# A causal-attention kernel on one core: the 512-column score product of heads 0 and 1 cut into 128 and 384 columns in all visits with a diagonal pair and one long product

## The chip, the cores and the metric

The kernel runs on one core of one Trainium2 chip. The metric is the device time of one execution in microseconds (us): the median of several runs. A core has these engines: TensorE for matrix products (PE, with its weight loads PEld), VectorE (DVE), ScalarE (ACT), GpSimd (POOL), and SyncE (SP), which issues transfers.

## The reference

The input x has 32 batches of 256 channels with 32 x 32 = 1024 tokens, in float32. Each batch is normalized over groups of 8 channels, projected to q, k and v of 8 heads with 32 channels each, and attended causally with the diagonal masked too; the result is added to x.

```python
q = einsum('oc,bcs->bos', q_w, xn) + q_b        # xn: x normalized by groups of 8 channels
k, v = split(einsum('oc,bcs->bos', kv_w, xn) + kv_b)
scores = einsum('bhqd,bhkd->bhqk', q, k) / sqrt(32)
attn = softmax(where(mask == 0, -10000, scores)) # mask: key strictly before query
out = x + einsum('bhqk,bhkd->bhqd', where(mask == 0, 0, attn), v)
```

## The kernel before

**Batches, groups, visits.** The 8 heads are two groups of four; a group's four heads lie in the four 32-row strips of a 128-row tile of q and of k. The 1024 tokens are 8 blocks of 128. For one batch and one group the causal half of the score matrix is cut into 6 visits (the table `VISITS`); a batch so has 12 visits, numbered v = 0 to 11, with the group g and the place i in the table as quotient and rest of v by 6. All 32 batches give 384 visits. A visit makes two sorts of score products, for keys on the rows of PSUM and queries on the columns:

- *long* ones, up to 512 columns, that need no mask. Visits 1 to 4 have one long product of 512 columns; visits 0 and 5 have two, of 384 and 128 columns.
- *short* ones. In visits 0, 1, 3 and 4 (the table `PAIRS`) this is a pair of diagonal blocks, in two phases: one of 128 columns and one of 64. In visits 2 and 5 it is one product of 256 columns.

**One row of products.** A product of one head has 32 rows of the array for its 32 channels. Each is made in two halves of 64 keys, which go to PSUM partitions 0 to 63 and 64 to 127. A row of the order of instructions, with "x4" at its end, is the product of two heads in both halves. Heads 0 and 1 are one pair and heads 2 and 3 the other: the two pairs lie in different strips of the array. As a product is in float32, the trace has two loads and two matmuls for it, which are called its two passes below; four records of the PE for each product.

**The order of a visit** is written by hand in `scores`, since all engines run under a manual schedule. With one long product and a pair of blocks it is: the short products of heads 2 and 3, the long one of heads 0 and 1, the long one of heads 2 and 3, a wait of PE for the semaphore `bank_free` (the short products of heads 2 and 3 have ended, whose PSUM banks the next write), and the short products of heads 0 and 1. Two lists set the first part:

- `begin` holds the calls that make the long products of heads 0 and 1. Where the visit is in the table `SPLIT` and the batch isn't the last, it holds two calls of `part_of`, for columns 0 to 127 and 128 to 511 of the one long product. `SPLIT` is compared with v, so it names visits 3 and 4 of group 0 alone.
- where `begin` has more than one call, its first is made between the two phases of the short products of heads 2 and 3, and these two phases come in reverse: 64 columns, the first call, 128 columns.

Behind the scores, PE makes a projection of this or the next batch (`project_qk` with tile `pp`, `project_v` with tile `ppv`) and then the products with v of the visit before (`values`, tile `acc`). ScalarE takes the exponential of the three pairs of PSUM banks (`sT`) into `e` and `eh`, GpSimd masks the diagonal blocks, VectorE adds up the exponentials by key. PSUM holds the score tiles three deep, two banks each, so each visit writes the banks that the visit before it wrote.

## Time and profile before

| | us |
|---|---|
| median of 3 runs (lowest, highest) | 1791.58 (1791.32, 1792.56) |
| span of the profiled execution, first to last instruction | 1791.2 |
| TensorE busy | 1782.1 (99%) |
| VectorE busy | 1669.4 (93%) |
| ScalarE busy | 1441.4 (80%) |
| GpSimd busy | 897.9 (50%) |

The page gives the span of the profiled execution and no separate time of its own; the span is 0.4 us less than the median of the runs. The granted clock of TensorE is 0.999 of the full one over the span. A line such as "912.56 1.46 PE L329 MATMUL sT<-q,k 32*64 32x64 f32 x56" of the timeline says: from 912.56 us on and for 1.46 us, 56 matmuls of line 329 one behind another, which write the tile sT from q and k, the first of them with 32 rows by 64 columns of weights and 64 streamed columns. Ends of matmuls are modelled, so the end of a row overlaps the next one; the starts don't. The time from the start of one sT row to the start of the row behind it is called the length of a section of scores here.

### The profile page before, as it was taken

To read this page: it belongs to the slowest core of one execution; us is meant where nothing else is said; L and a number is where in the kernel's file an instruction comes from. 1 tells how busy PE (TensorE), PEld (TensorE's weight loads), DVE (VectorE), ACT (ScalarE), POOL (GpSimd) and SP (SyncE) were. 2 spreads that over 40 slices of the span, in tenths; PEclk is the share of its full clock that TensorE was granted. 3 is DMA by queue.
4 is the path that set the end of the run, shared out by engine and by line. 5 is a ranking of instruction groups with operands and counts; after the bars stand their busy time and mean duration, and the time that the engine had idled before them with its cause. 6 is when DMAs were issued, how large, how long until landed. Compare 5 with 4: busy or idle time off the path is not lost.

```text
span 1791.2 us, 81784 instructions
## 1 busy us (share of the span) xinstructions
PE 1782.1 (99%) x37036; PEld 936.1 (52%) x37036; DVE 1669.4 (93%) x1796; ACT 1441.4 (80%) x1928; POOL 897.9 (50%) x935
## 2 busy tenths in 40 slices
PE   9999999999999999999999999999999999999998
PEld 5555555555555555555555555555555555555554
DVE  4689999999999999999999999999999999999998
ACT  6888878888778788788887888877888878888785
POOL 2355554554555555545555555454455554554542
PEclk9999999999999999999999999999999999999999
DMA  2567766767677676676776676767766766777663
GB/s 72 105 117 142 137 133 135 148 138 147 128 142 138 137 141 138 132 144 142 142 138 134 137 142 138 150 129 140 139 145 131 141 136 135 149 138 141 133 109 98
DMA packets 92771, 240.21 MB, mean 134 GB/s; under 512 B 26272, under 2 KB 27792, under 8 KB 76544
## 3 DMA queue, kind: packets, MB, share of 16 engines
q0 software_dynamic: 17360, 100.58, 40.1%
q1 hardware_dynamic: 74912, 134.28, 25.9%
q8 instruction: 290, 4.75, 1.1%
q14 instruction: 65, 0.53, 0.1%
q10 hardware_dynamic: 144, 0.07, 0.0%
HBM read 69.90 MB, written 34.95 MB: 59 GB/s over the span
## 4 chain that ended last, share of the span: by engine, by line
PE 99%; DVE 0%; ACT 0%; issue 0%; POOL 0%; POOLq 0%
PE sT L329 31%; PE acc L451 28%; PE pp L173 27%; PE ppv L173 13%; PE pd L503 1%; PE busy L159 0%; PE wt L152 0%; ACT e L426 0%; DVE rb_last L576 0%; DVE rb_last L563 0%; DVE turned L560 0%; DVE acc L573 0%; DVE inv_last L562 0%; POOL ident masks.py:199 0%; PE pv L173 0%
## 5 line engine op out<-in xcount | busy, mean ns | idle before, releaser
L426 ACT ACTIVATE e<-sT 128x1024 f32<-128x1024 f32 x768 | 744.3, 1022 | 301.5 <-PE sT L329 298.8
L366 POOL TENSOR_SCALAR_AFFINE_SELECT diagonal<-eh 128x512 f32<-128x512 f32 x512 | 563.3, 1122 | 625.4 <-ACT eh L422 624.7
L469 DVE TENSOR_TENSOR e<-e,e 128x1024 f32<-128x1024 f32 x314 | 578.0, 1841 | 23.0 <-ACT v L293 3.5
L329 PE MATMUL sT<-q,k 32*64 32x64 f32 (+1 forms) x18928 | 577.9, 367 | 0.1
L329 PEld LDWEIGHTS sT<-q,k 32*64 32x64 f32 x18928 | 397.0, 131 | 203.8 <-PE sT L329 67.4
L173 PE MATMUL pp<-xn,wT 128*32 128x512 f32 x4096 | 492.3, 598 | 0.0
L451 PE MATMUL acc<-e,v 128*32 128x512 f32 (+3 forms) x4608 | 401.0, 450 | 0.0
L422 ACT ACTIVATE eh<-sT 128x768 f32<-128x768 f32 (+1 forms) x384 | 341.6, 890 | 0.0
L451 PEld LDWEIGHTS acc<-e,v 128*32 128x32 f32 x4608 | 149.2, 110 | 261.5 <-issue 239.0
L173 PE MATMUL ppv<-wT,xn 128*32 128x256 f32 x4096 | 247.5, 382 | 0.0
L469 DVE TENSOR_TENSOR diagonal<-diagonal,e 128x1536 f32<-128x1536 f32 x126 | 194.5, 1544 | 16.1 <-PE acc L451 6.5
L173 PEld LDWEIGHTS pp<-xn,wT 128*32 128x32 f32 x4096 | 107.0, 109 | 195.8 <-issue 163.7
L469 DVE TENSOR_TENSOR e<-e,eh 128x1024 f32<-128x1024 f32 x126 | 177.6, 1410 | 6.5
L451 PEld LDWEIGHTS acc<-diagonal,v 128*32 128x32 f32 x4096 | 120.9, 110 | 88.1 <-issue 68.2
L173 PEld LDWEIGHTS ppv<-wT,xn 128*32 128x32 f32 x4096 | 120.2, 109 | 80.0 <-issue 7.0
L469 DVE TENSOR_TENSOR e<-e,diagonal 128x2048 f32<-128x2048 f32 x63 | 144.0, 2285 | 18.9 <-POOL diagonal L366 18.7
L451 PE MATMUL acc<-diagonal,v 128*32 128x128 f32 x4096 | 158.9, 273 | 0.0
L205 POOL DMA_INDIRECT eight<-each,group_of x31 | 42.9, 1383 | 193.4 <-DMA each<-st 193.4
L262 ACT ACTIVATE xn<-x,shift,rstd 128x256 f32<-128x256 f32 x248 | 137.2, 614 | 0.8 <-POOL shift L247 0.8
L576 DVE SCALAR_TENSOR_TENSOR rb<-num,v_bias_col,x 128x256 f32<-128x256 f32 x248 | 121.5, 530 | 4.4
L482 POOL DMA_DIRECT2D e<-e x124 | 103.6, 835 | 42.6 <-issue 42.6
L482 POOL DMA_DIRECT2D diagonal<-diagonal x124 | 105.1, 847 | 0.7
(87 smaller groups left out, 1092.2 us busy)
## 6 DMA issues: line engine op xcount, KB each, us to landing
x<-in_x_dram SPq DMA_DIRECT2D x124, 256.0 KB, 3.8
diagonal<-diagonal POOLq DMA_DIRECT2D x62, 512.0 KB, 6.1
e<-e POOLq DMA_DIRECT2D x62, 512.0 KB, 5.7
rb<-inverses SPq DMA_DIRECT2D x124, 256.0 KB, 4.0
out_dram<-rb SPq DMA_DIRECT2D x124, 256.0 KB, 4.2
diagonal<-diagonal POOLq DMA_DIRECT2D x62, 256.0 KB, 4.6
folded<-diagonal SPq DMA_DIRECT2D x62, 256.0 KB, 5.1
e<-e POOLq DMA_DIRECT2D x62, 256.0 KB, 4.6
```

What stands on the lines that cost most here:

```text
L173: nc.tensor.matmul(out[part], lhsT=lhsT[:, part], rhs=rhs, start=start, stop=stop, skip_group_check=True)
L205: nc.gpsimd.indirect_dma_start(eight, None, live["each", b].rearrange("(m c) s -> m (c s)", c=CPG), bass.IndirectOffsetOnAxis(ap=group_of[ ...
L262: nc.scalar.activation(to, of, AF.Identity, bias=live["shift", b][:, g : g + 1], scale=rstd)
L329: return nc.tensor.matmul(bank[c : c + KEYS, cols], lhsT=live["k", b, g][rows, kb * P + c : kb * P + c + KEYS], rhs=live["q", b, g][rows, ...
L366: nc.gpsimd.affine_select(out=square[:, :, place + s * P : place + (s + 1) * P], in_=raw[:, :, (1 - s) * KEYS : (3 - s) * KEYS], pattern=[ ...
L422: exp = nc.scalar.activation(eh.rearrange("p (n bank) q -> p bank n q", n=2)[:, :, :, :narrow], short[:, :, :, :narrow], AF.Exp)
L426: nc.scalar.activation(e[:, 2 * a : 2 * a + 2, :wide], pairs[a][:, :, :wide], AF.Exp)
L451: nc.tensor.matmul(acc[HD * j : HD * (j + 1), of], lhsT=live["v", b][:, kb, h * HD : (h + 1) * HD], rhs=e[:, j, :], start=first, stop=last ...
L469: nc.vector.tensor_add(to, to, tile_of(b, g, at))
L482: nc.gpsimd.dma_start(out=total[:rows], in_=total[rows : 2 * rows], accum_op=ALU.add)
L503: nc.tensor.matmul(pd[HD * j : HD * (j + 1), of], lhsT=pick, rhs=e[:, j, :], start=start, stop=stop, skip_group_check=True,)
L576: nc.vector.scalar_tensor_tensor(blocks(rb, s), blocks(num, s, (start + s) % 2 == 1), v_bias_col[:, g : g + 1], blocks(xt[:, g, cols], s), ...
```

## The change

`SPLIT` is now compared with i, the place in the table, and visit 1 is added. So visits 1, 3 and 4 of both groups have their long product of heads 0 and 1 in two pieces, in all batches but the last: in 31 batches, six visits each. And where a visit has one long product alone, the two phases of the pair are no longer in reverse: 128 columns, the first piece, 64 columns. Visit 0, with its two long products, keeps the reverse order.

```diff
-            if b < B - 1 and v in SPLIT:
+            if b < B - 1 and i in SPLIT:
                 begin = [lambda n=n: part_of(b, g, pairs[0], longs[0], n) for n in (slice(0, P), slice(P, HALF))]
             if i in PAIRS and len(begin) > 1:
-                first = short_of((2, 3), begin.pop(0), slice(None, None, -1))
+                first = short_of((2, 3), begin.pop(0), slice(None, None, -1 if len(longs) > 1 else 1))
             else:
                 first = short_of((2, 3))
...
-        SPLIT = 3, 4
+        SPLIT = 1, 3, 4
```

The first place is visit 1 of the first batch's group 0, on PE. The tiles sT_0_1_0, sT_0_1_1 and sT_0_1_2 hold the long products of heads 0 and 1, those of heads 2 and 3, and the short ones of all four. This is a piece of the difference:

```order
 L329 MATMUL sT_0_1_2_422<-q_0_284,k_0_295 64x128 x4
+L329 MATMUL sT_0_1_0_420<-q_0_284,k_0_295 64x128 x4
 L329 MATMUL sT_0_1_2_422<-q_0_284,k_0_295 64x64 x4
-L329 MATMUL sT_0_1_0_420<-q_0_284,k_0_295 64x512 x4
+L329 MATMUL sT_0_1_0_420<-q_0_284,k_0_295 64x384 x4
 L329 MATMUL sT_0_1_1_421<-q_0_284,k_0_295 64x512 x4
 L329 MATMUL sT_0_1_2_422<-q_0_284,k_0_295 64x128 x4
 L329 MATMUL sT_0_1_2_422<-q_0_284,k_0_295 64x64 x4
```

The row of 512 columns became one of 128, which moved between the two short rows of heads 2 and 3, and one of 384; the visit has one row more, and the order of the two short rows is as it was. Visits 1, 3 and 4 of group 1 change in the same way, and so do visits 1 of group 0 in the later batches.

The second place is visit 3 of group 0, which had two pieces before. PE before:

```order
L329 MATMUL sT_0_3_2_547<-q_0_284,k_0_295 64x64 x4
L329 MATMUL sT_0_3_0_545<-q_0_284,k_0_295 64x128 x4
L329 MATMUL sT_0_3_2_547<-q_0_284,k_0_295 64x128 x4
L329 MATMUL sT_0_3_0_545<-q_0_284,k_0_295 64x384 x4
L329 MATMUL sT_0_3_1_546<-q_0_284,k_0_295 64x512 x4
```

And PE now, at the same place:

```order
L329 MATMUL sT_0_3_2_551<-q_0_284,k_0_295 64x128 x4
L329 MATMUL sT_0_3_0_549<-q_0_284,k_0_295 64x128 x4
L329 MATMUL sT_0_3_2_551<-q_0_284,k_0_295 64x64 x4
L329 MATMUL sT_0_3_0_549<-q_0_284,k_0_295 64x384 x4
L329 MATMUL sT_0_3_1_550<-q_0_284,k_0_295 64x512 x4
```

Here the two short rows of heads 2 and 3, the first and the third, have changed places; nothing else moved. Visit 4 of group 0 changes in the same way. On the other engines the number of rows is the same in both kernels.

## The prediction

> **What bounds the kernel now.** I read the page first, for the engine that sets the end, then the groups by shape, then the timeline of PE over a batch, and last single instants inside two sections of scores.

> ```profile
> span 1791.2 us, 81784 instructions
> PE 1782.1 (99%) x37036; PEld 936.1 (52%) x37036; DVE 1669.4 (93%) x1796; ACT 1441.4 (80%) x1928; POOL 897.9 (50%) x935
> ...
> PE 99%; DVE 0%; ACT 0%; issue 0%; POOL 0%; POOLq 0%
> ...
> L426 ACT ACTIVATE e<-sT 128x1024 f32<-128x1024 f32 x768 | 744.3, 1022 | 301.5 <-PE sT L329 298.8
> ...
> L329 PE MATMUL sT<-q,k 32*64 32x64 f32 (+1 forms) x18928 | 577.9, 367 | 0.1
> L329 PEld LDWEIGHTS sT<-q,k 32*64 32x64 f32 x18928 | 397.0, 131 | 203.8 <-PE sT L329 67.4
> ```

> The chain that ends last is PE for 99% of the span, and the score matmuls wait 0.1 us in all: nothing feeds PE too late, so each ns of a section of scores is a ns of the kernel. ScalarE by contrast waits 298.8 us for these matmuls, over 384 visits 0.78 us each. A product leaves four records, two loads and two matmuls: 18928 of each kind.

> How long one matmul takes by its columns, from two groups of line 451 that nothing holds:

> ```profile
> L451 PE MATMUL acc<-e,v 128*32 128x512 f32 x1536 | 200.0, 592 | 0.0
> ...
> L451 PE MATMUL acc<-e,v 128*32 128x128 f32 x1024 | 51.4, 273 | 0.0
> ```

> That is (592 - 273) / 384 = 0.83 ns a column, and 273 - 128 x 0.83 = 167 ns that every record has on top. The second part overlaps the next matmul; the first doesn't, in one strip of the array.

> Now three sections of one batch: visit 1 of group 0 (one piece), visit 3 of group 0 (two pieces before too) and visit 3 of group 1 (one piece), each with the row behind it.

> ```profile
> 903.80 1.47 PE L329 MATMUL sT<-q,k 32*64 32x128 f32 x48
> 905.21 1.92 PE L173 MATMUL pp<-xn,wT 128*32 128x512 f32 x16
> ...
> 912.56 1.46 PE L329 MATMUL sT<-q,k 32*64 32x64 f32 x56
> 913.95 1.93 PE L173 MATMUL ppv<-wT,xn 128*32 128x256 f32 x32
> ...
> 940.03 1.47 PE L329 MATMUL sT<-q,k 32*64 32x128 f32 x48
> 941.43 1.93 PE L173 MATMUL ppv<-wT,xn 128*32 128x256 f32 x32
> ```

> Start to start that is 1.41 and 1.40 us with one piece, and 1.39 with two. So the trace of before already holds the experiment: of a split with the 64 columns first. Each pair of heads streams 512 + 128 + 64 = 704 columns twice, 704 x 2 x 0.83 = 1.17 us. The sections are longer than that by 0.22 to 0.23 us, and much shorter than the 2.34 us of both pairs one after the other: the pairs do run side by side. What keeps a split section at 1.39?

> **The hold.** In the section that starts at 912.56, I number the products 1 to 28 in the order of the program: 1 to 4 (64 columns, heads 2 and 3), 5 to 8 (128, heads 0 and 1), 9 to 12 (128, heads 2 and 3), 13 to 16 (384, heads 0 and 1), 17 to 20 (512, heads 2 and 3), and so on. Below are the loads that run at 912.899 and at 913.009 (the first number is the start of the oldest), then the 128- and 64-column matmuls recorded at 912.870, and the 128-column ones at 912.905, when no 64-column one is left.

> ```profile
> 912.84 0.17 PEld L329 LDWEIGHTS sT<-q,k 32*64 32x64 f32 x5
> ...
> 912.91 0.22 PEld L329 LDWEIGHTS sT<-q,k 32*64 32x64 f32 x7
> ...
> L329 PE MATMUL sT<-q,k 32*64 32x128 f32 x16 | 0.5, 281 | 0.0
> ...
> L329 PE MATMUL sT<-q,k 32*64 32x64 f32 x4 | 0.2, 217 | 0.0
> ...
> L329 PE MATMUL sT<-q,k 32*64 32x128 f32 x15 | 0.5, 278 | 0.0
> ```

> At 912.899 five loads run: four are the second loads of products 13 to 16, and one is the first load of product 17, from 912.84 on. Products 18 to 20 have the same strips and shape, and their loads don't follow; the next load of all begins at 912.91. What ended shortly before? The second matmuls of products 1 to 4: four are recorded at 912.870 and none at 912.905, and as four loads or matmuls of a row follow each other within 0.02 us, product 1 ended at about 912.88. Some 0.03 us later product 18 was let in. I read it as a queue that holds 16 products, 64 records, and gives up places in order, when a product has ended: product 17's first load takes the place of product 1's first load, and product 18 has to wait for the end of product 1, 19 for that of 2, 20 for that of 3.

> The wait costs something because products 17 to 20 are the next work of heads 2 and 3. Counts of score matmuls recorded at three instants later in that section:

> ```profile
> 913.36:913.37 0.01, 0.01 (x8) 1.00 9.71 1638
> ...
> 913.40:913.41 0.01, 0.01 (x10) 1.00 0.00 0
> 913.42:913.43 0.01, 0.01 (x12) 1.00 0.00 0
> ```

> No score matmul ends in these 0.07 us, so the four that come on top are the second matmuls of products 17 to 20: two by 913.40, the last by 913.43. The last therefore streams from 0.87 us after the section's start to 0.87 + 512 x 0.00083 = 1.295, and the next row starts at 1.39, 0.095 later.

> A second place tells what ends the hold. Visit 0 of group 1 (from 926.71 on) has as its last row 64 columns of heads 0 and 1; 16 products ahead of it lie the 384 columns of heads 0 and 1. The matmuls recorded at 927.800 and 927.832, and the oldest load that runs at 927.930:

> ```profile
> L329 PE MATMUL sT<-q,k 32*64 32x384 f32 x8 | 0.6, 481 | 0.0
> L329 PE MATMUL sT<-q,k 32*64 32x128 f32 x12 | 0.4, 268 | 0.0
> ...
> L329 PE MATMUL sT<-q,k 32*64 32x384 f32 x4 | 0.5, 481 | 0.0
> L329 PE MATMUL sT<-q,k 32*64 32x128 f32 x12 | 0.4, 268 | 0.0
> ...
> 927.84 0.22 PEld L329 LDWEIGHTS sT<-q,k 32*64 32x64 f32 x7
> ```

> Four of the eight 384-column matmuls ended between the two instants, and a load began at 927.84: the same order of events, with another shape and at another time in the section.

> **The change part by part.** *The sections that are split anew.* Each of the 124 (31 batches, four visits) loses a row of 512 columns and gets one of 128 and one of 384: the same columns, four products and so eight matmuls and eight loads more. The columns are streamed at the same rate and cost nothing; a load is hidden where the matmul ahead of it in its strip is longer than it. What counts is that the row of 512 columns of heads 2 and 3 now begins with the 17th product, not the 13th. In the one-piece section it was among the first 16 and not held.

> *The order of the short rows.* In all 186 sections product 1 now has 128 columns, where the old split has 64. Its end comes 2 x 64 x 0.83 = 106 ns later: not at 912.88 - 912.56 = 0.32 us after the section's start, but at 0.43. So product 18 is let in at 0.46, not 0.35. Nothing makes up for it: heads 2 and 3 have streamed their 192 short columns by the same time in either order, and have nothing else to do. The last product's second matmul starts at 0.87 + 0.106 = 0.976 and ends at 1.40; with the 0.095 behind it the section takes 1.495 us. Heads 0 and 1 aren't held and end, as in the old split, no later than 1.295, so heads 2 and 3 decide.

> *The sum.* The 62 sections split before go from 1.39 to 1.495: 62 x 0.106 = 6.6 us. The 124 new ones go from 1.405 (mean of the two rows) to 1.495: 124 x 0.09 = 11.2 us. Together 17.8. Against the span of 1791.2 this gives 1809.0, and the runs' median is 0.4 above the span: 1809.4.

> *What the trace doesn't show.* No section of before begins with 128 columns and is split, so the hold's end is extrapolated. Low end: the three held products come as close together as loads do where nothing holds them, so that the last loses 0.03 less; the section takes 1.465, the sum is 62 x 0.076 + 124 x 0.06 = 12, and the time 1804. High end: the 0.03 from the end of a product to the load is paid twice: 1.525, 62 x 0.136 + 124 x 0.12 = 23, 1815. I take the middle, since both places showed the same 0.03.

> *Edits that I cost at nothing.* The exponential of heads 2 and 3 starts some 0.1 us later; ScalarE's 0.78 us of waiting per visit covers it. PE's wait for `bank_free` is for the short rows of heads 2 and 3, which have ended in either order before the 512-column rows are through. GpSimd and VectorE get more time per visit, not less.

> [...]

> **The rivals.** *One: no new cost.* The hold doesn't hang on product 1 but on something that keeps its place, such as the first matmuls of heads 0 and 1 (128 columns): of the sixteen 128-column records at 912.870 one had gone by 912.905 too. Then all 186 sections take 1.39: 124 x 0.015 = 1.9 us less, 1789.7. If the hold were gone altogether, heads 0 and 1 would end the section, at about 1.38: 124 x 0.025 + 62 x 0.01 = 3.7 less, 1787.9. It decides from the point where the loads of products 18 to 20 come by 0.36. Against it stands the second place: the count of 128-column matmuls is 12 at both instants there, so no such matmul ended before that load. Chance 0.11.

> *Two: the pairs run free.* With each short row opposite a piece of equal or greater length, the two pairs take 704 columns each from the start and the section 1.17 + 0.11 = 1.28 us: 124 x 0.125 + 62 x 0.11 = 22 less, 1769. For it stands that the strips do stream side by side; against it that the old split, which has the same columns opposite each other, takes 1.39. Chance 0.03. [...]

> *Three: the lateness spreads.* The exponentials of heads 2 and 3 free their banks too late for the next visit, and PE waits there too. At 0.1 us more in 186 visits this is 1828. It takes ScalarE's cover to be gone, and PE's 0.1 us of waiting in all shows none of it. Chance 0.02.

> **How the numbers follow.** The forecast, with its own range of 1804 to 1815, has 0.84; about 0.8 of the whole lies inside that range, so it needs no widening to the rivals. A measurement of this kernel can tell about 0.2%, 3.6 us, from no change. Slower by more: the forecast and the third rival, 0.86. Within: nearly all of the first rival, 0.10. Faster by more: the second rival and the far end of the first, 0.04.

> **What would show it.** Right: the sections of visits 1, 3 and 4 last about 1.49 us in both groups; in a split section the last second matmul of 512 columns starts near 0.98 us; the loads of products 18 to 20 begin 0.03 us after product 1 has ended, near 0.46; sections of visits 0, 2 and 5 stay as they are; PE's count grows by 992 to 38028. Wrong: sections of 1.38 to 1.39 (first rival), under 1.3 (second), or a score matmul that waits for ScalarE (third).

## The result and the profile after

| | before | after |
|---|---|---|
| median of 4 runs, us | 1791.65 | 1817.53 |
| lowest to highest | 1791.32 to 1792.56 | 1817.27 to 1819.79 |
| ratio, 95% interval | 1 | 1.0148 (1.0134 to 1.0161) |

The change makes the kernel slower by 25.9 us. The forecast was 1809.4 with a range of 1804 to 1815: the right sign, but the time lies 2.5 us above the range. The page of the changed kernel:

```profile
span 1815.8 us, 83768 instructions
PE 1802.8 (99%) x38028; PEld 960.8 (53%) x38028; DVE 1661.3 (91%) x1796; ACT 1444.1 (80%) x1928; POOL 874.2 (48%) x935
...
q8 instruction: 298, 4.88, 1.1%
...
PE 98%; issue 1%; DVE 0%; DMA 0%; ACT 0%; SPq 0%
```

PE has the 992 matmuls more that were forecast, and is still what sets the end. But it is busy for 13 us less than the span, where it was 9 us less before, and "issue", which had 0% of the chain, has 1%. That entry is PE standing still with nothing in the profile to wait for. Queue q8 brings in instructions; it has 298 packets now and had 290:

```profile
q8 instruction: 290, 4.75, 1.1%
```

The same three sections as in the prediction, visit 1 and visit 3 of group 0 and visit 3 of group 1, each with the row behind it:

```profile
914.37 1.56 PE L329 MATMUL sT<-q,k 32*64 32x128 f32 x56
915.86 1.92 PE L173 MATMUL pp<-xn,wT 128*32 128x512 f32 x16
...
923.22 1.56 PE L329 MATMUL sT<-q,k 32*64 32x128 f32 x56
924.71 1.93 PE L173 MATMUL ppv<-wT,xn 128*32 128x256 f32 x32
...
950.98 1.56 PE L329 MATMUL sT<-q,k 32*64 32x128 f32 x56
952.48 1.93 PE L173 MATMUL ppv<-wT,xn 128*32 128x256 f32 x32
```

Start to start 1.49, 1.49 and 1.50 us: the sections are as long as forecast. The hold shows in the section that starts at 923.22. The loads that run at 923.736, and the 128-column matmuls recorded at 923.640 and at 923.668:

```profile
923.67 0.19 PEld L329 LDWEIGHTS sT<-q,k 32*64 32x64 f32 x4
...
L329 PE MATMUL sT<-q,k 32*64 32x128 f32 x8 | 0.3, 268 | 0.0
...
L329 PE MATMUL sT<-q,k 32*64 32x128 f32 x4 | 0.3, 268 | 0.0
```

Four of the eight 128-column matmuls, the second ones of products 1 to 4, end between the two instants, and the load of product 18 begins at 923.67: 0.45 to 0.46 us after the section's start, where 0.46 was forecast.

What was not forecast is in single sections, such as visit 1 of group 0 in batch 9:

```profile
522.66 1.56 PE L329 MATMUL sT<-q,k 32*64 32x128 f32 x53
524.68 0.33 PE L329 MATMUL sT<-q,k 32*64 32x64 f32 x3 [0.46 <-issue]
524.94 1.50 PE L173 MATMUL pp<-xn,wT 128*32 128x512 f32 x12
```

This section takes 2.28 us. PE stops inside its last row of products, where nothing is waited for, and goes on 0.8 us later.

I worked out from the starts of all sections and rows in the trace, kind by kind, the usual (median) time of each and what single ones take over it, counting those that are over 0.04 us longer as stalls. Before: 3 stalls, 1.1 us in all; in the longest, 0.7 us, the late loads wait for ScalarE, in the other two for GpSimd's mask. After: 13 stalls, 8.1 us, of another sort, as the experiments show. The 186 sections: 62 x 0.103 + 124 x 0.088 = 17.3 us, since they take 1.491 and took 1.388 and 1.403. From the first section of the first batch to that of the last, 1707.6 us became 1732.8: 25.2 more, of which 17.3 are the sections, 7.0 the stalls, and 0.9 lie in smaller pieces.

### The profile page after: what moved, and what is told of

It is laid out like the page before. It is cut to its first block, busy times and chain, and to the rows that moved or that the text cites. A ratio compares the mean times of both kernels' runs of the same rounds, so it can differ in the third digit from the quotient of the medians.

```text
span 1815.8 us, 83768 instructions
## 1 busy us (share of the span) xinstructions
PE 1802.8 (99%) x38028; PEld 960.8 (53%) x38028; DVE 1661.3 (91%) x1796; ACT 1444.1 (80%) x1928; POOL 874.2 (48%) x935
## 3 DMA queue, kind: packets, MB, share of 16 engines
q1 hardware_dynamic: 74912, 134.28, 25.5%
q8 instruction: 298, 4.88, 1.1%
## 4 chain that ended last, share of the span: by engine, by line
PE 98%; issue 1%; DVE 0%; DMA 0%; ACT 0%; SPq 0%
PE sT L329 30%; PE acc L451 27%; PE pp L173 27%; PE ppv L173 14%; PE pd L503 1%; DMA x<-in_x_dram 0%; PE wt L152 0%; ACT e L426 0%; DVE st L189 0%; DVE rb_last L576 0%; ACT xn L262 0%; DVE rb_last L563 0%; PE busy L159 0%; SPq L111 0%; DVE turned L560 0%
## 5 line engine op out<-in xcount | busy, mean ns | idle before, releaser
L426 ACT ACTIVATE e<-sT 128x1024 f32<-128x1024 f32 x768 | 744.5, 1021 | 321.4 <-PE sT L329 319.9
L366 POOL TENSOR_SCALAR_AFFINE_SELECT diagonal<-eh 128x512 f32<-128x512 f32 x512 | 538.1, 1072 | 671.3 <-ACT eh L422 671.0
L329 PE MATMUL sT<-q,k 32*64 32x64 f32 (+1 forms) x19920 | 598.5, 358 | 3.4 <-issue 3.2
L469 DVE TENSOR_TENSOR e<-e,e 128x1024 f32<-128x1024 f32 x314 | 569.1, 1813 | 22.9 <-PE acc L451 3.4
L329 PEld LDWEIGHTS sT<-q,k 32*64 32x64 f32 x19920 | 421.1, 131 | 183.5 <-issue 49.1
L173 PE MATMUL pp<-xn,wT 128*32 128x512 f32 x4096 | 493.5, 598 | 0.4 <-ACT xn L262 0.4
L451 PE MATMUL acc<-e,v 128*32 128x512 f32 (+3 forms) x4608 | 401.9, 450 | 0.0
L451 PEld LDWEIGHTS acc<-e,v 128*32 128x32 f32 x4608 | 150.1, 110 | 261.2 <-issue 237.1
L173 PE MATMUL ppv<-wT,xn 128*32 128x256 f32 x4096 | 247.5, 382 | 0.0
L173 PEld LDWEIGHTS pp<-xn,wT 128*32 128x32 f32 x4096 | 107.3, 109 | 206.7 <-issue 181.7
L451 PEld LDWEIGHTS acc<-diagonal,v 128*32 128x32 f32 x4096 | 121.8, 110 | 87.5 <-issue 67.9
L173 PEld LDWEIGHTS ppv<-wT,xn 128*32 128x32 f32 x4096 | 120.3, 109 | 89.7 <-issue 23.4
L451 PE MATMUL acc<-diagonal,v 128*32 128x128 f32 x4096 | 159.6, 273 | 0.0
```

The source lines that it names most:

```text
L173: nc.tensor.matmul(out[part], lhsT=lhsT[:, part], rhs=rhs, start=start, stop=stop, skip_group_check=True)
L329: return nc.tensor.matmul(bank[c : c + KEYS, cols], lhsT=live["k", b, g][rows, kb * P + c : kb * P + c + KEYS], rhs=live["q", b, g][rows, ...
L366: nc.gpsimd.affine_select(out=square[:, :, place + s * P : place + (s + 1) * P], in_=raw[:, :, (1 - s) * KEYS : (3 - s) * KEYS], pattern=[ ...
L426: nc.scalar.activation(e[:, 2 * a : 2 * a + 2, :wide], pairs[a][:, :, :wide], AF.Exp)
L451: nc.tensor.matmul(acc[HD * j : HD * (j + 1), of], lhsT=live["v", b][:, kb, h * HD : (h + 1) * HD], rhs=e[:, j, :], start=first, stop=last ...
L469: nc.vector.tensor_add(to, to, tile_of(b, g, at))
```

## The experiments

Two theories stand for the two parts. **Hold:** products 18 to 20 of a section wait for the end of products 1 to 3 (in the section of before that starts at 912.56 product 1 ends at 912.88 and the load of product 18 begins at 912.91; in that of after at 923.22 it is 923.645 and 923.675). I read this as PE taking in 16 products at a time and giving up places in order. **Fetch:** PE's instructions come in fetches of equal size. 38028 matmuls and as many loads in 298 packets are 255 instructions each; each packet has 16384 bytes in the trace (4.88 MB in 298), and with the few other instructions of PE I take it as 256, an estimate that the places of the stops bear out below. One batch in each kernel, before and after (from the first section of batch 16 to that of batch 17, so that a few records of the row ahead are counted too):

```profile
899.23:954.21 54.98, 54.98 (x1156) 28.86 (x1152) 52.69 (x57) 44.94 (x60) 28.78 (x29) 1.00 0.70 139
```

```profile
909.81:965.34 55.53, 55.53 (x1188) 29.64 (x1184) 52.89 (x57) 44.99 (x60) 28.73 (x29) 1.00 0.67 134
```

1152 loads, and as many matmuls, are 2304 instructions, 9 fetches; 1184 of each are 2368, 9.25 fetches. (Two semaphore instructions of line 796 per batch come on top in both.) So before, each fetch falls at nearly the same place of every batch, and now the places move by a quarter of a fetch from batch to batch. The packets show it: in batches 4 to 9 the fifth packet starts 25.5 to 26.1 us after the batch does before, and 25.9 to 32.7 us now. By the theory, a fetch that meets other transfers comes late and PE runs dry.

| kernel | ratio (95%) | the split sections, us | fetches per batch | stalls: number, us |
|---|---|---|---|---|
| before | 1 | 1.39 | 9 | 3, 1.1 |
| order_only | 1.0034 (1.0022 to 1.0045) | 1.49 | 9 | 3, 1.4 |
| after | 1.0148 (1.0134 to 1.0161) | 1.49 | 9.25 | 13, 8.1 |
| split_only | 1.0052 (1.0036 to 1.0069) | 1.39 | 9.25 | 22, 10.6 |
| before_64 | 1.0063 (1.0047 to 1.0080) | 1.39 | 9.25 | 28, 11.0 |
| piece64 | 1.0145 (1.0127 to 1.0164) | 1.49 | 9.25 | 22, 10.0 |
| swap | 1.0249 (1.0230 to 1.0268) | 1.61 | 9.25 | 21, 6.6 |
| after_192 | 1.0104 (1.0087 to 1.0121) | 1.49 | 10 | 8, 3.9 |
| split_192 | 1.0004 (0.9995 to 1.0013) | 1.39 | 10 | 10, 1.7 |
| no_fold | 1.0084 (1.0068 to 1.0101) | 1.49 | 9.25 | 0, 0.0 |

The stalls are those of the one profiled execution of each. In the kernels with many stalls another way of cutting the rows changes their number by up to 3 and their sum by up to 0.8 us. In order_only, after_192 and split_192 the longest one (0.7 to 1.0 us) is in the very first visit, before the loop of batches has settled.

**order_only**: the order of the phases alone, against before.

```diff
-                first = short_of((2, 3), begin.pop(0), slice(None, None, -1))
+                first = short_of((2, 3), begin.pop(0), slice(None, None, -1 if len(longs) > 1 else 1))
```

> Only the order of the two phases is changed, in the 62 sections that are split already. Hold theory: these last 1.49 instead of 1.39 us, 62 x 0.103 = 6.4 us more, the others stay. Fetch theory: the number of PE instructions per batch is that of before, so no new stalls, near 1798 us. Rival (stalls belong to the long sections): a third of the long sections, so a third of the stalls, near 1800.5 us.

Measured: 1799.64 us against 1793.34 of before, measured beside it, 6.3 more. Visit 1 of group 0, which isn't split, and visit 3, which is:

```profile
906.81 1.47 PE L329 MATMUL sT<-q,k 32*64 32x128 f32 x48
908.21 1.93 PE L173 MATMUL pp<-xn,wT 128*32 128x512 f32 x16
...
915.57 1.56 PE L329 MATMUL sT<-q,k 32*64 32x128 f32 x56
917.06 1.93 PE L173 MATMUL ppv<-wT,xn 128*32 128x256 f32 x32
```

1.40 as before, and 1.49. The order of two rows with the same columns costs 0.10 us a section, as the hold theory has it, and the stalls are as few as before.

**split_only**: the split everywhere, 64 columns first, against after.

```diff
-                first = short_of((2, 3), begin.pop(0), slice(None, None, -1 if len(longs) > 1 else 1))
+                first = short_of((2, 3), begin.pop(0), slice(None, None, -1))
```

> Visits 1, 3 and 4 of both groups are split, but the 64-column phase stays ahead of the 128-column one. Hold theory (product 18 waits for the end of product 1): product 1 has 64 columns again, so all 186 sections last 1.39 us, as the old split ones; 124 x 0.015 = 1.9 us less in sections. Fetch theory (the PE instructions of a batch no longer make whole fetches of 256, so the fetches wander through the batch and PE runs dry where they meet other transfers): stalls of 0.2 to 1.5 us in single sections stay, some 8 us in all, near 1797.5 us. Rival (the stalls belong to the long sections): no stalls, near 1789.7 us.

Measured: 1801.83 us, 8.5 over before. The sections take 1.387 us, those of visit 4 of group 0 mostly some more, with small stalls in many batches. What the split gains in the sections, some 2 us, is lost five times over: the stalls don't need the long sections. About 4 us of them lie on that visit 4 and are partly of another sort, which after_192 shows.

**before_64**: the kernel before, with two projections of a batch in halves.

```diff
+            halves = 2 if b and (g, hf) == (0, 0) else 1
+            for part in (slice(HALF // halves * k, HALF // halves * (k + 1)) for k in range(halves)):
                 for cc in range(NG):
                     product(
-                    pp, wT[:, cc, n * C + g * P : n * C + (g + 1) * P], live["xn", b, hf][:, cc, :],
+                        pp[:, part], wT[:, cc, n * C + g * P : n * C + (g + 1) * P], live["xn", b, hf][:, cc, part],
```

> The kernel before, with two of the 512-column projections of each batch made as two halves of 256 columns: the same columns, 16 products and so 64 PE instructions more per batch, the sections of scores as before. Fetch theory: fetches wander as in the changed kernel, single stalls of 0.2 to 1.5 us, some 8 us in all, near 1799.5 us. Rival (stalls belong to the long sections, or to the score products): none, near 1791.7 us.

Measured: 1804.51 us, 11.2 over before, with not one score product changed. Visit 3 of group 0 in batch 16 and, as an example of a stall, visit 10 of batch 22:

```profile
917.61 1.46 PE L331 MATMUL sT<-q,k 32*64 32x64 f32 x56
919.00 0.85 PE L173 MATMUL ppv<-wT,xn 128*32 128x256 f32 x12
...
1282.95 0.56 PE L331 MATMUL sT<-q,k 32*64 32x128 f32 x15
1284.28 1.42 PE L331 MATMUL sT<-q,k 32*64 32x64 f32 x33 [0.77 <-issue]
1285.63 0.64 PE L173 MATMUL pp<-xn,wT 128*32 128x512 f32 x4
```

The section of 1.39 us is that of before. The other one takes 2.68: PE stops in the middle of it. Sixty-four PE instructions more per batch are enough, in the projections as in the scores. The rival, stalls that belong to the long sections, falls. Of the 11 us, 3.3 lie on visit 4 of group 0, again partly of the other sort.

**after_192**: the changed kernel, with six projections in halves, which fills the batch up to 10 fetches.

```diff
+            halves = 2 if b and (g, hf) != (1, 1) else 1
```

> The changed kernel, with six of the eight projections of a batch in two halves: 192 PE instructions more per batch, which makes whole fetches again (64 + 192 = 256). Hold theory: sections stay at 1.49 us, 17.2 us above the kernel before. Fetch theory: no wandering, so either no stalls, near 1809 us, or one at the same place of every batch. Rival (stalls belong to the long sections): the stalls stay, near 1817.5 us.

Measured: 1812.09 us, ratio 1.0104 where the changed kernel has 1.0148. It has more instructions, and is faster than the changed kernel. Half of the stalls are gone rather than all, but what is left is mostly of another sort. One, of 0.9 us, is in the very first visit. Five, 2.2 us, fall on visit 4 of group 0. At least four of them don't stand where a fetch ends (how that is seen is told below): PE stops there near the first products of the 512-column row and goes on after GpSimd's indirect transfer of line 205 has ended, 0.5 to 0.9 us into the section; in the other batches that transfer ends by 0.2, and there is no such stall. That transfer alone isn't the cause, since in the changed kernel it ends as late (0.53) in two batches without a stall; what holds PE there isn't shown. Only two stalls, 0.8 us in all, stand at the end of a fetch, where the changed kernel has 8.1 us. So the fetch theory's choice of one bad place isn't what happened: with whole fetches nearly all stalls of that kind are gone.

**no_fold**: the changed kernel without GpSimd's adding transfers.

```diff
-            nc.gpsimd.dma_start(out=total[:rows], in_=total[rows : 2 * rows], accum_op=ALU.add)
+            return
```

> The changed kernel without the adding transfers of GpSimd's queue (the folds of the sums over the rows of keys, 512 and 256 KB each), so the sums hold a quarter of the rows only: this part of the computation is left out. PE's instructions and their number per batch (9.25 fetches) are those of the changed kernel, sections of 1.49 us. Fetch theory (a fetch is late because it stands behind other transfers): nearly no stalls left, 0 to 2 us instead of 8, near 1810 us. Rival (PE runs dry wherever a fetch falls at certain places of a batch, whatever else is transferred): stalls as in the changed kernel, near 1817.5 us.

Measured: 1806.80 us against 1791.67. No section or row of the trace is over 0.04 us longer than its kind. The engines on its page, GpSimd's queue (q0) and that of the instructions:

```profile
PE 1798.2 (100%) x38028; PEld 959.4 (53%) x38028; DVE 1653.0 (92%) x1796; ACT 1443.7 (80%) x1928; POOL 645.7 (36%) x687
...
q0 software_dynamic: 1488, 3.05, 0.6%
...
q8 instruction: 298, 4.88, 1.1%
```

The same 38028 matmuls, the same 298 fetches, the same wandering, and not one stall: it takes both, a fetch at a bad place and GpSimd's adding transfers. From the first to the last batch this kernel takes 1723.8 us, 16.2 over before: the 17.3 of the sections less the 1.1 of stalls of before. Its last batch is 2 us shorter as well, which is why the time lies below the expected 1810.

How a fetch and a stall stand to each other can be seen at the stall of 523.9 in the changed kernel. The queues from 519 to 522 us and from 522 to 524 us:

```profile
q1 hardware_dynamic: 133, 0.42, 49.0%
q0 software_dynamic: 40, 0.20, 37.7%
```

```profile
q1 hardware_dynamic: 55, 0.10, 14.2%
q8 instruction: 1, 0.02, 2.9%
q0 software_dynamic: 1, 0.00, 0.0%
```

For three microseconds SyncE's and GpSimd's transfers take 87% of the DMA engines, and no instructions come. Then the others thin out, one packet of instructions is moved (it starts at 522.24, 9.4 us after the one before it, where the middle of the gaps in the kernel before is 6.0), and PE goes on at 524.68, 1.5 us after the packet has ended.

That this is the cause in general can be counted. I numbered all records of PE in a trace (loads, matmuls and its few other instructions) by their starts. In all ten kernels together, between 25 and 1760 us, there are 27 gaps of more than 0.55 us between one start and the next: 8 in the changed kernel, 5 in split_only, 6 in before_64, 1 in after_192, 5 in piece64, 2 in swap, none in the other four. Every one of the 27 ends at a record whose number leaves 193 when it is divided by 256, and 1.2 to 1.6 us after a packet of instructions has landed. So PE stops where one fetch ends and the next begins, 256 apart, and a wait for data or for another engine would not keep to these places. All 13 stalls of the changed kernel, the small ones too, have such a record in them or right behind them, 1.2 to 1.6 us after its packet. In no_fold, over the same stretch, no such record comes sooner than 2.36 us after its packet; in the kernel before the middle is 4.2 us, two of 284 come sooner than 1.6, and none of its three stalls is at such a record.

The size of a fetch agrees with these places: 4.88 MB in 298 packets, 16 KB each, and stops 256 records apart. In the kernel before, with 290 packets of the same size, none of the 1.1 us of stalls is at a fetch; in the changed kernel, whose fetches wander among transfers that take 87% of the engines in the stretch above, all 8.1 us are.

**swap**: the changed kernel with the 512-column row of heads 2 and 3 ahead of the 384-column row of heads 0 and 1 (the batch stays at 9.25 fetches).

```diff
+            late = begin.pop() if i in PAIRS and len(longs) == 1 and b < B - 1 else None
             for f in begin:
                 f()
             long_of((2, 3), 0)
+            if late:
+                late()
```

> The changed kernel with the 512-column row of heads 2 and 3 ahead of the 384-column row of heads 0 and 1 in the six split visits, so that the latter has products 17 to 20. Hold theory: now the 384 columns of heads 0 and 1 are let in at 0.46 us instead of 0.30, and as heads 0 and 1 have 192 more columns behind them, the section lasts about 1.61 us: 186 x 0.12 = 22 us over the changed kernel, near 1840 us. Rival (the delay belongs to the 512-column row of heads 2 and 3 wherever it stands, or to the 128-column phase coming first): sections of 1.49 us or less, 1817 us or less.

Measured: 1839.43 us against 1793.61. Visit 3 of group 0:

```profile
934.52 1.68 PE L329 MATMUL sT<-q,k 32*64 32x128 f32 x56
936.13 1.07 PE L173 MATMUL ppv<-wT,xn 128*32 128x256 f32 x16
```

1.61 us, as the hold theory says to the hundredth: whichever row has products 17 to 20 is late, and with heads 0 and 1 it is the dearer one. The rival, a delay of the 512-column row wherever it stands, falls.

**piece64**: the changed kernel with pieces of 64 and 448 columns.

```diff
-                begin = [lambda n=n: part_of(b, g, pairs[0], longs[0], n) for n in (slice(0, P), slice(P, HALF))]
+                begin = [lambda n=n: part_of(b, g, pairs[0], longs[0], n) for n in (slice(0, KEYS), slice(KEYS, HALF))]
```

> The changed kernel with pieces of 64 and 448 columns in place of 128 and 384. Hold theory (product 1, of 128 columns, must have ended): nothing changes, sections of 1.49 us, near 1817 us. Rival (the hold ends with the first piece of heads 0 and 1, products 5 to 8, whose passes are now 53 ns shorter each): sections of 1.38 to 1.44 us, near 1800 to 1808 us.

Measured: 1820.83 us, ratio 1.0145, sections of 1.492 us. The size of the first piece doesn't matter, so the hold doesn't end with the first products of heads 0 and 1, which was the prediction's first rival.

**split_192**: split_only with the projections of after_192.

> A candidate for a faster kernel: the split everywhere with the 64-column phase first, and six projections of a batch in halves so that the PE instructions of a batch make whole fetches. Hold theory: sections of 1.39 us, 124 x 0.016 = 2.0 us less than before; the halves cost 1.5 us (P sections of after_192 against before). Fetch theory: few stalls, as in after_192, 1 to 4 us. Together 0.5 to 3.5 us above the kernel before, ratio 1.000 to 1.002. If the stalls don't go with the whole fetches: some 10 us, ratio 1.005.

Measured: 1794.83 us against 1793.61, ratio 1.0004 with 1 inside the interval. The sections take 1.387 us (1.388 in visit 4 of group 1), but for ten that are longer, most of them on visit 4 of group 0; the stalls come to 1.7 us. This is the split that the old sections promised, and what it gains, 2.0 us, goes to the halves and the stalls. It beats the changed kernel, and doesn't beat the kernel before.

## Why the prediction was partly right and where it failed

*What bounds the kernel, and the hold:* right. The sections take 1.491 us where 1.495 was forecast, the load of product 18 comes at 0.46, and the sum of 17.8 us measured 17.3. order_only, swap and piece64 each tell it from one of its rivals.

*The middle of the bounds:* right. The 0.03 us from the end of a product to the load stayed (product 1 ends at 923.645 and the load of product 18 begins at 923.675, where before it was 912.881 and 912.912), and neither end of the range was reached.

*The edits costed at nothing:* ScalarE's cover held, and no section of scores is longer than the hold and the stalls make it. One reading was too broad: the 0.1 us that the score matmuls wait in all counts only time in which PE had nothing running. A section of before, visit 11 of batch 10, was already 0.7 us longer than its kind because its loads waited for ScalarE.

*The step that failed* is in the part on the sections split anew: "The columns are streamed at the same rate and cost nothing; a load is hidden where the matmul ahead of it in its strip is longer than it." In the sections that held: those split anew, with eight loads and eight matmuls more, take 1.387 us in split_only where they took 1.403 before. But it prices the time of the 64 instructions more per batch and not their coming in. They turn 9 fetches per batch into 9.25, and that is 7.0 us of stalls which the sum didn't have: 17.3 + 7.0 + 0.9 is the 25.2 of the trace. before_64 shows this cost without a change to the scores, no_fold takes all of it away, and after_192 takes the stalls at a fetch from 8.1 us to 0.8. The page of before could have raised the question: its q8 line has 290 packets for 74072 instructions, and the counts of a batch give 9 fetches without a rest.

*A smaller slip:* the median was taken as the span and 0.4 us. In the ten runs of before measured beside order_only each time is 1.7 to 1.8 us above its own span. So the profiled execution of before, with a span of 1791.2, took an estimated 1792.9, and the 0.4 compared two different executions. Its 1.1 us of stalls may then not be in the usual run: without them the span would be 1790.1, and 1790.1 + 17.3 + 8.1 + 1.8 = 1817.3 comes near the median of after, 1817.53 (its profiled execution took 1817.61 with a span of 1815.8, hence the 1.8).

*The rivals:* the first (no new cost) falls with the sections of 1.49 and piece64; the second (free pairs) with the same; the third (lateness that spreads to ScalarE) has no sign in the trace: all 13 stalls are at a fetch. None of the three rivals had the cost that came on top.

Open is why the bad place lies where it does. That PE stops at the end of a fetch is counted above, one fetch overdue behind 87% busy DMA engines is seen in the trace, and no_fold shows that GpSimd's transfers are needed for it; which transfer holds which fetch wasn't measured. Open too are the stalls on visit 4 of group 0 in split_only, before_64 and after_192 that aren't at a fetch; the changed kernel has none of them.

## What to carry to other kernels

Before rows of products are reordered, look in the trace for a load that comes late and for the matmul that ends just before it: a piece put between two others moves everything behind it, and here products 18 to 20 of a section waited for products 1 to 3 to end (0.03 us from the end of the first to the load), so that the shorter row belonged first (0.10 us a section in order_only). When an edit adds instructions to an engine that is always busy, compare the count per turn of the loop with the instructions of one fetch in the trace (256 here); a whole number of fetches (9 or 10 a batch) kept them in place in these runs, with 0.8 us of stalls at fetches or less, and a rest (9.25) made them wander, which cost several us as long as GpSimd's adding transfers ran. A split that adds no streamed column cost more in instructions here than it saved in streaming: in split_only some 2 us were gained in the sections, and the time rose by 8.5.
